# A four-layer gated cross-attention and FFN kernel on one core: packed rest matmuls, one-hot routing tile by tile, and two shared-expert tiles moved among the expert blocks

## The chip, the cores and the metric

The kernel runs on one core of a Trainium2 chip, in one launch. The metric is device time in microseconds (us). Beside unprofiled runs there is one profiled execution with a trace of every engine: PE (TensorE matmuls), PEld (TensorE weight loads, which overlap PE), DVE (VectorE), ACT (ScalarE), POOL (GpSimd) and SP, which only issues DMAs.

## The reference, cut to what matters

The stream x is 1024 tokens of 256 floats, eight tiles of 128 tokens. Four layers each add a gated attention and a gated FFN to it. All arithmetic is fp32 unless said otherwise. What the change touches is the attention of layer 0 and the expert FFNs of layers 0 and 3:

```
# layer 0 attention: 16 heads, rotary queries of 192, latent keys of 64
q_big  = rope((x @ Wq.T) per head @ w_kc_q)       # 192 a head
q_r    = q_big @ W_qr[h];  k_r = kv_r @ W_kr[h]   # 64 a head
x     += tanh(g) * (softmax(q_r @ k_r.T) @ kv_r @ w_kc_kv.T @ Wo.T)

# layer 0 FFN: 16 experts, 6 a token, and a shared expert
probs  = softmax(x @ gate_w.T);  idx = top_k(probs + gate_b, 6)
y      = sum over the chosen e of probs[e] * (silu(x@W1e.T+b1e) * (x@W3e.T+b3e)) @ W2e.T + ...
z      = silu(x @ ws1.T + bs1) * (x @ ws3.T + bs3) @ ws2.T + bs2
x     += tanh(g) * (y + z)

# layer 3 FFN: 8 experts, 2 a token, and a shared expert, without biases
```

## The kernel before, in words

**Queues.** Every engine executes its instructions in the order in which the built program holds them. That order comes from a scheduler: it follows the program text roughly, and it moves an operation ahead where it expects its inputs early. PSUM has two pools, `mm` (four banks) and `wide` (two pairs of banks).

**Layer 0's projections** (`attention0`, L647). `fold_scores0` (L468) multiplies W_qr and W_kr of each head into a matrix from the 192 rotary columns to the 64 latent ones, and splits it: `wide` holds the first 64 columns of each rotary half, `rest` the last 32, with zeros beside them, so that two heads share 128 output columns. The loop at L711 goes over four head groups f and two token groups g (eight units of three steps). `rotated(n)` multiplies xT by folded query weights (L407, four matmuls of 128x128 by 512), DVE multiplies by the rotary tables (L668), POOL adds (L676, L677). `to_latent(u)` (L680) applies `wide` in eight 64x64 matmuls. `rest_to_latent(u)` (L697) applies `rest` in four matmuls of 64 rows by 128 columns, and ACT copies the sums to SBUF.

**Layer 0's FFN** (`ffn0`, L1263). After two layernorms the normalised rows go to DRAM (`xd0`). `routing` (L1271) is a generator whose steps are taken between pieces of the shared expert: gate softmax and top six (`chosen`, L934), then `placed` (L985), which gives every (token, expert) pair a slot in blocks of 128 slots for one expert each. Its last part turns slots into token numbers with one-hot matrices: for each of the six picks DVE makes a hit matrix for all eight tiles at once (L1055, L1062, L1068, L1071), and PE adds them up in eight fp16 matmuls of 126 columns (L1073). From the sum DVE makes the gather and scatter indices (L1085 to L1089).

The shared expert runs over the eight tiles in three stages, `up` (L1283), `turn` (L1302), `down` (L1309), as `in_three` (L1256) staggers them; each tile ends in `gated_add` to x. Then `keep_rows` writes x to a sum in DRAM, `sums0[0]`.

**The blocks** (`Experts`, L1119; 55 in layer 0, 20 in layer 3). In iteration i, POOL gathers the rows of block i + 4 (`fetch`, L1137), PE transposes block i (`turn`, L1149), transposes the hidden of block i - 2 (L1204), does `up` of i - 1 (L1174, L1178, in layer 3 L1189) and `down` of i - 2 (L1213), and POOL scatters the result of i - 2 into one of two sums by turns, with addition in the DMA (L1225). Then `between(i)` puts other work in: every third block from i = 2 a step of `fold1` (L742, the folding of layer 1's attention weights: two steps at L753, one at L771, four at L784, four at L564, and a last one that only frees buffers), and after that steps of `ternary1` (L1439, DVE work for layer 1's FFN weights).

**Weights** pass through three buffers `C`; `used(name)` (L245) frees one and SP issues the load of the next.

**After the blocks** x is read back from `sums0[0]` in eight DMAs of 128 KB on SP, the other sum in four of 256 KB on ACT's queue, and DVE adds them (L1361) before layer 1's layernorm. At the end of the kernel the last sum is copied to the output in four DMAs (L1609).

## Time and profile before

| | |
|---|---|
| three runs | 974.55, 975.81, 976.93 us; median 975.81 |
| profiled execution | 984.07 us, of which the trace spans 982.3 |
| busy: PE, PEld, DVE, ACT, POOL | 860.7, 557.0, 527.7, 274.0, 343.7 us |
| mean granted PE clock | 0.931 of full speed |
| DMA | 75.12 MB in 40426 packets, mean 76 GB/s |

The stages that the change touches, in us from the span's start, read from the timeline:

| stage | from | to |
|---|---|---|
| layer 0's projections (`attention0`, the loop at L711) | 17 | 153 |
| shared expert and routing (`ffn0`) | 221 | 277 |
| layer 0's blocks, first gather to last scatter issued | 270.12 | 465.09 |
| reload of x, to layer 1's first transpose | 469.14 | 482.22 |
| layer 3's FFN, shared expert and blocks | 796 | 973 |
| copy to the output | 975.70 | 982.3 |

How to read it: a time is the busy time of one engine, and an idle engine costs nothing unless the others wait for it. A timeline row has start, duration, engine, source line, operation, output and inputs with their shapes, count, and in brackets the idle time before it and what ended that. A matmul of fp32 operands appears as two records; the end of a matmul is modelled, so the distance from one group's start to the next group's start is more reliable than a duration.

### The profile page before, as it was taken

How to read it: one execution, taken by the hardware profiler on the slowest of the kernel's cores; microseconds unless marked ns; L12 is line 12 of the kernel's file. 1: busy time of each engine (PE TensorE's matmuls, PEld its weight loads, DVE VectorE, ACT ScalarE, POOL GpSimd, SP SyncE). 2: the span in 40 equal slices, each digit the busy share in tenths (PEclk: the TensorE clock that was granted, in tenths of full speed). 3: DMA queues.
4: the chain of work that ended last, by engine and by line, in shares of the span. 5: the costliest groups of instructions: out<-in, count | busy, mean ns of one | idle time of the engine just before them, and what ended most of it. 6: DMA issues, size and time to landing. Idle time of an engine off the chain costs nothing.

```text
span 982.3 us, 12516 instructions
## 1 busy us (share of the span) xinstructions
PE 860.7 (88%) x4389; PEld 557.0 (57%) x4389; DVE 527.7 (54%) x1261; ACT 274.0 (28%) x531; POOL 343.7 (35%) x260
## 2 busy tenths in 40 slices
PE   5999998999999998985399988988637889999994
PEld 3544335876767876763247863745424656566662
DVE  3656455756934445461427748958786846222220
ACT  2211013334222232221113437024303532122221
POOL 0445451310067786786003127104101302144421
PEclk9999999999989999998599999979858979999998
DMA  9200217301166667555720000440000011122222
GB/s 354 81 15 11 88 34 232 89 22 30 54 156 163 126 151 168 80 84 64 245 99 1 1 1 27 162 144 1 22 0 1 2 43 51 44 44 44 39 27 60
DMA packets 40426, 75.12 MB, mean 76 GB/s; under 512 B 6369, under 2 KB 28883, under 8 KB 38987
## 3 DMA queue, kind: packets, MB, share of 16 engines
q1 hardware_dynamic: 24426, 51.99, 15.7%
q0 software_dynamic: 14496, 20.47, 12.8%
q10 hardware_dynamic: 1440, 1.84, 0.5%
q8 instruction: 39, 0.64, 0.3%
q14 instruction: 25, 0.20, 0.1%
HBM read 58.70 MB, written 16.61 MB: 77 GB/s over the span
## 4 chain that ended last, share of the span: by engine, by line
PE 34%; DVE 11%; ACT 3%; POOL 1%; issue 1%; DMA 1%; POOLq 0%; ACTq 0%; DVEq 0%
PE wide L1189 7%; PE mm L407 5%; PE mm L1213 3%; PE wide L1389 3%; PE mm L642 2%; PE mm L1520 2%; PE mm L437 2%; PE mm L915 1%; PE mm L1410 1%; PE mm L392 1%; DVE mx L884 1%; DVE big L1436 1%; PE wide L873 1%; DVE attn L886 1%; DVE sm L421 1%; DVE big L1437 1%
## 5 line engine op out<-in xcount | busy, mean ns | idle before, releaser
L423 POOL TENSOR_TENSOR attn<-attn,sm 128x1024 f32<-128x1024 f32 x32 | 60.8, 1901 | 245.8 <-DVE sm L422 227.2
L1198 DVE SCALAR_TENSOR_TENSOR blk<-wide,weight,blk 128x176 f32<-128x176 f32 (+1 forms) x75 | 37.0, 493 | 133.6 <-ACT blk L1197 130.7
L1225 POOL DMA_INDIRECT sums<-ring,big x55 | 87.8, 1596 | 32.1 <-issue 15.7
L668 DVE TENSOR_TENSOR rope<-wide,big 128x512 f32<-128x512 f32 x96 | 59.6, 684 | 57.1 <-PE wide L407 55.6
L407 PE MATMUL wide<-xT,big 128*128 128x512 f32 x192 | 88.6, 609 | 0.3 <-ACT big L542 0.3
L1178 PE MATMUL wide<-big,blk 128*128 x220 | 76.5, 469 | 0.0
L1137 POOL DMA_INDIRECT xs<-xd,big x55 | 54.8, 997 | 55.4 <-PE mm L1318 35.8
L1189 PE MATMUL wide<-big,blk 128*128 x160 | 72.2, 593 | 0.5 <-DVE blk L1150 0.5
L392 PE MATMUL mm<-ident,xn 128*128 128x128 f32 x112 | 24.7, 376 | 53.4 <-DVE xn L380 41.1
L1197 ACT ACTIVATE blk<-wide 128x176 f32<-128x176 f32 (+1 forms) x75 | 29.4, 392 | 121.8 <-PE wide L1189 60.2
L407 PEld LDWEIGHTS wide<-xT,big 128*128 128x128 f32 x192 | 35.6, 193 | 48.5 <-issue 38.7
L642 PE MATMUL mm<-vo,attnT 128*128 128x256 f32 x256 | 60.5, 390 | 0.9 <-ACT attnT L438 0.9
L1213 PE MATMUL mm<-big,blk 88*128 x220 | 57.7, 385 | 0.8 <-ACT blk L1206 0.5
L642 PEld LDWEIGHTS mm<-vo,attnT 128*128 128x128 f32 x256 | 48.5, 195 | 9.5 <-ACT attnT L438 3.3
L392 PEld LDWEIGHTS mm<-ident,xn 128*128 128x128 f32 x112 | 18.2, 189 | 62.3 <-ACT rstd L375 31.7
L438 ACT COPY attnT<-mm 128x512 f32<-128x512 f32 x64 | 35.0, 588 | 66.2 <-PE mm L437 66.2
L1213 PEld LDWEIGHTS mm<-big,blk 88*128 88x128 f32 x220 | 41.9, 192 | 16.7 <-ACT blk L1206 1.5
L1178 PEld LDWEIGHTS wide<-big,blk 128*128 128x128 f32 x220 | 40.3, 194 | 12.9 <-issue 0.8
L437 PE MATMUL mm<-ident,attn 128*128 128x128 f32 x256 | 36.9, 292 | 11.5 <-POOL attn L423 11.5
L442 DVE SCALAR_TENSOR_TENSOR x<-mm,tg,x 128x256 f32<-128x256 f32 x48 | 22.9, 477 | 44.7 <-PE mm L642 19.8
L421 DVE TENSOR_REDUCE sm<-attn 128x16 f32<-128x1024 f32 x32 | 38.9, 1215 | 14.7 <-ACT attn L415 12.6
L1137 POOL DMA_INDIRECT xs<-xd,scratch x20 | 19.4, 972 | 76.9 <-PE mm L1149 51.9
(330 smaller groups left out, 1690.4 us busy)
## 6 DMA issues: line engine op xcount, KB each, us to landing
big<-in_L_w_gate_up SPq DMA_DIRECT2D x8, 1024.0 KB
big<-in_L_w SPq DMA_DIRECT2D x4, 1408.0 KB
big<-in_L_w_down SPq DMA_DIRECT2D x8, 512.0 KB
w_L_qk<-in_L_qk SPq DMA_DIRECT2D x4, 896.0 KB
big<-in_L_w SPq DMA_DIRECT2D x4, 704.0 KB
big<-in_L_wo SPq DMA_DIRECT2D x1, 2048.0 KB
xd<-xn SPq DMA_DIRECT2D x16, 128.0 KB
sums<-x SPq DMA_DIRECT2D x16, 128.0 KB
```

The costliest lines, as they stand in the source:

```text
L392: nc.tensor.transpose(ps[:, i * P : (i + 1) * P], n[:, c * P : (c + 1) * P], ident)
L407: nc.tensor.matmul(ps, w(c), xT[:, c, :], start=(c == 0), stop=(c == 1))
L421: nc.vector.tensor_reduce(sm, e, AX.X, ALU.add)
L423: nc.gpsimd.tensor_tensor(e, e, sm.unsqueeze(2).to_broadcast([P, groups, n]), ALU.mult)
L437: nc.tensor.transpose(ps[:, i * P : (i + 1) * P], ev[:, pr * P : (pr + 1) * P], ident)
L642: nc.tensor.matmul(ps[:, :D], aT[:, s, :], vo[:, s, :], start=(s == 0), stop=(s == NP - 1))
L668: nc.vector.tensor_tensor(m[:, s, :].rearrange("q (b t) -> q b t", t=S), ps[:, s, :].rearrange("q (b t) -> q b t", t=S), table, ALU.mult,)
L1137: nc.gpsimd.indirect_dma_start(out=xs, out_offset=None, in_=self.xd, in_offset=bass.IndirectOffsetOnAxis(ap=self.gather[:, b : b + 1].bitc ...
L1178: nc.tensor.matmul(ps[:, 0, : 2 * n], st[:, c * P : (c + 1) * P], self.w[:, bass.ds(r + c * 2 * n, 2 * n)], start=False, stop=(c == 1),)
L1189: nc.tensor.matmul(ps[:, k, :n], st[:, c * P : (c + 1) * P], self.w[:, bass.ds(r + (2 * c + k) * n, n)], start=(c == 0), stop=(c == 1),)
L1213: nc.tensor.matmul(ps[:, :D], hT[:, j * P : (j + 1) * P], self.w[: self.chunk, bass.ds(r + j * D, D)], start=(j == 0), stop=(j == self.n - 1),
L1225: nc.gpsimd.indirect_dma_start(out=self.sums[b % len(self.sums)], out_offset=bass.IndirectOffsetOnAxis(ap=self.scatter[:, b : b + 1].bitca ...
```

## The change

It has five parts.

1. `rest` loses its zero half. Both token groups of one f now run together: `rest_to_latent(f)` issues 16 matmuls of 32 rows by 64 columns, at eight places of the array, into four PSUM banks. For token group 1 the two heads of a pair change places in the 128 latent rows (`half = i ^ g`), and the values of the second half of the tokens are stored swapped to match. The six steps of one f are taken in the order `turns`.
2. The hit matrices are made tile by tile: one TENSOR_SCALAR for the slot's row, one that compares the block and multiplies by the token number (up to 1024, in fp16). The one-hot matmuls have 63 columns.
3. The last two of the eight shared tiles are issued among blocks 1 to 6, one piece (`up`, `turn` or `down`) a block; their results are kept in SBUF (`later`) and added after the blocks. The folding's steps start at block 10 instead of 2, the ternary steps after block 45, two a block. L0_s13 and L0_s2 are freed after the last shared piece.
4. x is one tile of SBUF. In layer 0 the rows in DRAM are ordered with the eight tokens of one partition side by side, so that x and the second sum come back in two DMAs each with 4 KB pieces, and DVE adds 512 columns at once.
5. The output copy's access pattern has rows of 4 KB.

```diff
-        for n in range(3 * len(units) + 2):
+        turns = [(0, 0), (1, 0), (2, 0), (2, 1), (0, 1), (1, 1)]
...
+        for n in range(6 * NQ + 2):
+            f, m = divmod(n, 6)
...
+            if m == 3 and f < NQ:
+                to_latent(f, 0)
+            if m == 5:
+                rest_to_latent(f)
+            if m == 1 and f >= 1:
+                to_latent(f - 1, 1)
...
-        def rest_to_latent(u):
-            f, g = units[u]
-            pss, qr = sums.pop(u), made.pop(3 * u + 2)
+        def rest_to_latent(f):
+            sums[f, 1] = [ps_mm() for _ in range(2)]
+            qrs = [made.pop(6 * f + 2 + g) for g in range(NG)]
             for s in range(2):
-                for up in range(2):
-                    rows = slice(up * 64, (up + 1) * 64)
-                    nc.tensor.matmul(pss[up], rest[rows, f, s, :], qr[rows, s, :], start=False, stop=(s == 1))
+                for g in range(NG):
+                    for i in range(2):
+                        for up in range(2):
+                            lo, half = up * 64 + i * 32, i ^ g
+                            nc.tensor.matmul(
+                                sums[f, g][up][half * DC : (half + 1) * DC, :],
+                                rest[lo : lo + 32, f, s, :],
+                                qrs[g][lo : lo + 32, s, :],
+                                start=(s == 0 and g == 1),
+                                stop=(s == 1 and g == 0),
+                                tile_position=(lo, half * DC),
+                            )
...
-            nc.vector.tensor_tensor(
-                h,
-                place.unsqueeze(1).to_broadcast([P, NT, P]),
-                off[:, ts].unsqueeze(2).to_broadcast([P, NT, P]),
-                ALU.is_equal,
-            )
...
+            for t in range(NT):
+                m = k * NT + t
+                nc.vector.tensor_scalar(h[:, t, :], place, off[:, m : m + 1], None, ALU.is_equal)
+                nc.vector.tensor_scalar(
+                    v[:, t, :], block16[:, :nb], blk[:, m : m + 1], number[:, t : t + 1], ALU.is_equal, ALU.mult
+                )
...
+            if t < LATER:
+                gated_add(t, ps[:, :D], gate)
+            else:
+                nc.vector.tensor_scalar(later[:, t - LATER, :], ps[:, :D], gate, None, ALU.mult)
...
-        in_three(NT, up, turn, down)
+        in_three(LATER, up, turn, down)
...
         def between(i):
-            if i % 3 == 2 and not ended:
+            if shared:
+                if i:
+                    f, t = shared.pop(0)
+                    f(t)
+                if not shared:
+                    used("L0_s13")
+                    used("L0_s2")
+            elif i > 9 and i % 3 == 1 and not ended:
...
-            if i > 32 and ended:
+            for _ in range(2 if ended and i > 45 else 0):
                 next(ternary, None)
...
         for t in range(NT):
-            nc.sync.dma_start(out=x[t], in_=sums0[0][t * P : (t + 1) * P, :])
+            if t % TPG == 0:
+                tiles = slice(t, t + TPG)
+                nc.sync.dma_start(out=stream[:, tiles, :], in_=tiled(sums0[0], 0)[:, tiles, :])
+                more = t4([P, TPG, D], "more")
+                nc.scalar.dma_start(out=more, in_=tiled(sums0[1], 0)[:, tiles, :])
             if t % 2 == 0:
...
+                done = nc.vector.tensor_tensor(stream[:, two, :], stream[:, two, :], more[:, its, :], ALU.add)
+                if t >= LATER:
+                    mine = slice(t - LATER, t - LATER + 2)
+                    done = nc.vector.tensor_tensor(stream[:, two, :], stream[:, two, :], later[:, mine, :], ALU.add)
```

More of the change, by code (lines that the diff above doesn't have):

```diff
@@ L59 @@
 K3 = 2
+LATER = 6
 def _blocks(experts, keep):
@@ L76 @@
 C_SLOTS = 3
-FIXED = 2 * DC + 8 + 2 * E0 + E0 + 8 + 2 * E3 + 4 + 1 + NB0 + 8 + 1 + L + 2 + 1
-FIXED16 = P + NT + P + E0 * E0
+FIXED = 2 * DC + 8 + 2 * E0 + E0 + 8 + 2 * E3 + 4 + NB0 + 8 + 2 * NT + 1 + L + 2 + 1
+FIXED16 = P + NB0 + P + E0 * E0
 @with_exitstack
@@ L134, in evacuate @@
             nc.vector.tensor_copy(dst, src)
-    x = [const.tile([P, D], F32, tag=f"x{t}", name=f"x{t}") for t in range(NT)]
+    stream = const.tile([P, NT, D], F32, tag="x", name="x")
+    x = [stream[:, t, :] for t in range(NT)]
     big = const.tile([P, BIG], F32, tag="big", name="big")
@@ L174, in tile_flamingo @@
     which = take(4)
-    row1 = take(1)
     block = take(NB0)
     full = take(8)
+    number0, number3 = take(NT), take(NT)
     expert_of = take(1)[:96]
@@ L183, in tile_flamingo @@
     place = take(P, left16)
-    tile_of = take(NT, left16)
+    block16 = take(NB0, left16)
     before = take(P, left16)
@@ L359, in zeroed, with tiled, keep_rows @@
         nc.sync.dma_start(out=rows.rearrange("(p r) d -> p (r d)", p=P), in_=zeros[:, : rows.shape[0] * D // P])
-    def keep_rows(sums):
+    def tiled(rows, layer):
+        order = "(p t) d -> p t d" if layer == 0 else "(t p) d -> p t d"
+        return rows[:T].rearrange(order, t=NT)
+    def keep_rows(sums, layer):
         for t in range(NT):
-            nc.sync.dma_start(out=sums[t * P : (t + 1) * P, :], in_=x[t])
+            nc.sync.dma_start(out=tiled(sums, layer)[:, t, :], in_=x[t])
     def layernorm(g):
@@ L473, in fold_scores0 @@
         wide = wqk[:, :1024].rearrange("p (f i s d) -> p f i s d", f=NQ, i=2, s=2)
-        rest = wqk[:, 1024:].rearrange("p (f s i d) -> p f s i d", f=NQ, s=2, i=2)
-        nc.gpsimd.memset(rest, 0.0)
+        rest = wqk[:, 1024:1536].rearrange("p (f s d) -> p f s d", f=NQ, s=2)
         rT = w_rk0[:, : NP * CQ].rearrange("r (h q) -> r h q", h=NP)
@@ L516, in fold_scores0 @@
                     evacuate(
-                        rest[rows, fs, :, i, :],
+                        rest[rows, fs],
                         rests[up][rows, :256].rearrange("p (f s d) -> p f s d", f=2, s=2),
                     )
-        return wide, rest.rearrange("p f s i d -> p f s (i d)")
+        return wide, rest
     def fold_queries0(f):
@@ L594, in latents, with latent_attend @@
         return [t[:, g] for g in range(NG)]
-    def latent_attend(qcT, wvo, gate):
+    def latent_attend(qcT, wvo, gate, swapped=False):
         vos: dict = {}
@@ L616, in values @@
                 for j, ps in enumerate(pss):
-                    evacuate(v[:, 2 * r : 2 * r + 2, j, :], ps.rearrange("p (q o) -> p q o", q=2))
+                    evacuate(v[:, 2 * r : 2 * r + 2, (1 - j) if swapped and b >= B // 2 else j, :], ps.rearrange("p (q o) -> p q o", q=2))
             vos[b] = v.rearrange("p q j o -> p (q j) o")
@@ L652, in attention0 @@
         ring = region("weff", 2048, "rotated").rearrange("p (i s t) -> p i s t", i=2, s=2)
-        units = [(f, g) for f in range(NQ) for g in range(NG)]
+        turns = [(0, 0), (1, 0), (2, 0), (2, 1), (0, 1), (1, 1)]
         made: dict = {}
@@ L657, in rotated @@
         def rotated(n):
-            u, k = divmod(n, 3)
-            f, g = units[u]
+            f, m = divmod(n, 6)
+            k, g = turns[m]
             ps = ps_wide()
@@ L678, in rotated, with to_latent @@
             made[n] = qr
-        def to_latent(u):
-            f, _ = units[u]
-            pss = sums[u] = [ps_mm() for _ in range(2)]
-            qrs = [made.pop(3 * u + i) for i in range(2)]
+        def to_latent(f, g):
+            if not g:
+                sums[f, g] = [ps_mm() for _ in range(2)]
+            pss = sums[f, g]
+            qrs = [made.pop(6 * f + 4 * g + i) for i in range(2)]
             for s in range(2):
                 for i in range(2):
+                    half = i ^ g
                     for up in range(2):
@@ L689, in to_latent, with finished @@
                         nc.tensor.matmul(
-                            pss[up][i * DC : (i + 1) * DC, :],
+                            pss[up][half * DC : (half + 1) * DC, :],
                             wide[rows, f, i, s, :],
                             qrs[i][rows, s, :],
-                            start=(s == 0),
-                            stop=False,
-                        )
-        def rest_to_latent(u):
-            f, g = units[u]
-            pss, qr = sums.pop(u), made.pop(3 * u + 2)
-            for s in range(2):
-                for up in range(2):
-                    rows = slice(up * 64, (up + 1) * 64)
-                    nc.tensor.matmul(pss[up], rest[rows, f, s, :], qr[rows, s, :], start=False, stop=(s == 1))
-            for up in range(2):
-                last.append(nc.scalar.copy(qcT[g][:, 2 * f + up, :], pss[up]))
+                            start=(s == 0 and g == 0),
+                            stop=(s == 1 and g == 1),
+                        )
+            if g:
+                finished(f, g)
+        def rest_to_latent(f):
+            sums[f, 1] = [ps_mm() for _ in range(2)]
+            qrs = [made.pop(6 * f + 2 + g) for g in range(NG)]
+            for s in range(2):
+                for g in range(NG):
[10 more added lines that the diff above has]
+                            )
+            finished(f, 0)
+        def finished(f, g):
+            for up, ps in enumerate(sums.pop((f, g))):
+                last.append(nc.scalar.copy(qcT[g][:, 2 * f + up, :], ps))
         wide = None
@@ L710, in attention0 @@
         output = fold_output(w_kv0, [lambda: (w_o0, NH, lambda: None)])
-        for n in range(3 * len(units) + 2):
-            u, k = divmod(n, 3)
-            if n == 1:
+        for n in range(6 * NQ + 2):
+            f, m = divmod(n, 6)
+            if n == 2:
                 xT.append(transposed(layernorm(1)))
-            if u < len(units):
+            if f < NQ:
                 rotated(n)
-                if k == 1 and u % 2 == 0 and u // 2 + 1 < NQ:
-                    fold_queries0(u // 2 + 1)
-                if k == 1 and u >= len(units) - 4:
+                if m == 1 and f + 1 < NQ:
+                    fold_queries0(f + 1)
+                if m % 3 == 1 and f >= NQ - 2:
                     next(output)
@@ L722, in attention0 @@
                 wide, rest = fold_scores0()
-            if k == 0 and u >= 1:
-                to_latent(u - 1)
-            if k == 1 and u >= 1:
-                rest_to_latent(u - 1)
+            if m == 3 and f < NQ:
[4 more added lines that the diff above has]
+                to_latent(f - 1, 1)
             if n >= 6:
@@ L738, in attention0 @@
             load_experts0(e, e + 4)
-        latent_attend(qcT, wvo, gate)
+        latent_attend(qcT, wvo, gate, swapped=True)
         load_experts0(12, 16)
@@ L983, in chosen, with placed @@
         return cw, gated, mask
-    def placed(mask, n, keep, nb, stride, cut, keeping):
+    def placed(mask, n, keep, nb, stride, number, cut, keeping):
         order = [cut([P, NT, 8 + n]) for _ in range(2)]
@@ L1048, in placed @@
         hit = [cut([P, NT, P], F16) for _ in range(2)]
-        val = [cut([P, NT, 2, nb], F16) for _ in range(2)]
+        val = [cut([P, NT, nb], F16) for _ in range(2)]
         ps = ps_mm()
-        src = ps[:, : 2 * nb]
+        src = ps[:, :nb]
         for k in range(keep):
             h, v = hit[k % 2], val[k % 2]
-            ts = slice(k * NT, (k + 1) * NT)
-            nc.vector.tensor_tensor(
-                h,
-                place.unsqueeze(1).to_broadcast([P, NT, P]),
-                off[:, ts].unsqueeze(2).to_broadcast([P, NT, P]),
-                ALU.is_equal,
-            )
-            is_in = v[:, :, 0, :]
-            nc.vector.tensor_tensor(
-                is_in,
-                block[:, :nb].unsqueeze(1).to_broadcast([P, NT, nb]),
-                blk[:, ts].unsqueeze(2).to_broadcast([P, NT, nb]),
-                ALU.is_equal,
-            )
-            nc.vector.tensor_tensor(
-                v[:, :, 1, :], is_in, tile_of.unsqueeze(2).to_broadcast([P, NT, nb]), ALU.mult
-            )
-            nc.vector.tensor_scalar(is_in, is_in, row1, None, ALU.mult)
+            for t in range(NT):
[4 more added lines that the diff above has]
+                )
             for t in range(NT):
@@ L1075, in placed @@
                     h[:, t, :],
-                    v[:, t].rearrange("p a b -> p (a b)"),
+                    v[:, t],
                     start=(k == 0 and t == 0),
@@ L1080, in placed @@
             yield
-        row = cut([P, nb])
         none = cut([P, nb])
@@ L1084, in placed @@
         gather = keeping([P, nb], I32)
-        nc.vector.tensor_copy(row, src[:, :nb])
-        nc.vector.scalar_tensor_tensor(row, src[:, nb:], float(P), row, ALU.mult, ALU.add)
-        nc.vector.tensor_scalar(none, row, 0.0, spare, ALU.is_equal, ALU.mult)
-        nc.vector.scalar_tensor_tensor(scatter, row, -1.0, none, ALU.add, ALU.add)
+        nc.vector.tensor_scalar(none, src, 0.0, spare, ALU.is_equal, ALU.mult)
+        nc.vector.scalar_tensor_tensor(scatter, src, -1.0, none, ALU.add, ALU.add)
         nc.vector.tensor_scalar(gather, scatter, T - 1, None, ALU.bitwise_and)
@@ L1105, in placed, with stored @@
         return gather, scatter, expert, offset, used_blocks
-    def stored(normal, name, n):
-        xd = dram.tile([T, D + n], F32, tag=name, name=name)
+    def stored(normal, layer, n):
+        xd = dram.tile([T, D + n], F32, tag=f"xd{layer}", name=f"xd{layer}")
         for g, xn in enumerate(normal):
@@ L1112, in stored, with with_weights @@
                 t = g * TPG + i
-                nc.sync.dma_start(out=xd[t * P : (t + 1) * P, :D], in_=n)
+                nc.sync.dma_start(out=tiled(xd, layer)[:, t, :D], in_=n)
         return xd
-    def with_weights(xd, gated):
-        nc.sync.dma_start(out=xd[:, D:].rearrange("(t p) e -> p t e", p=P), in_=gated)
+    def with_weights(xd, layer, gated):
+        nc.sync.dma_start(out=tiled(xd, layer)[:, :, D:], in_=gated)
     class Experts:
@@ L1265, in ffn0 @@
         xT = [xt for xt, _ in normal]
-        xd = stored([xn for _, xn in normal], "xd0", E0)
+        xd = stored([xn for _, xn in normal], 0, E0)
         work, places = big[:, X0W : BIG - 400], Carver(big[:, BIG - 400 :])
@@ L1273, in routing @@
             route.append(cw)
-            with_weights(xd, gated)
-            route.append((yield from placed(mask, E0, K0, NB0, W0, cut, places)))
+            with_weights(xd, 0, gated)
+            route.append((yield from placed(mask, E0, K0, NB0, W0, number0, cut, places)))
         steps = routing()
@@ L1321, in down @@
             nc.tensor.matmul(ps[:, :D], cwT, b2_0, start=False, stop=True)
-            gated_add(t, ps[:, :D], gate)
-        in_three(NT, up, turn, down)
+            if t < LATER:
[3 more added lines that the diff above has]
+        in_three(LATER, up, turn, down)
         for _ in steps:
             pass
-        used("L0_s13")
-        used("L0_s2")
-        keep_rows(sums0[0])
+        keep_rows(sums0[0], 0)
         placing = route[1]
@@ L1336, in hTs @@
             return st[:FC0, 432:688]
+        later = work[:, : (NT - LATER) * D].rearrange("p (t d) -> p t d", d=D)
         fold = fold1()
@@ L1340, in ffn0 @@
         ternary = ternary1()
+        shared = [(f, t) for t in range(LATER, NT) for f in (up, turn, down)]
         def between(i):
-            if i % 3 == 2 and not ended:
+            if shared:
[6 more added lines that the diff above has]
+            elif i > 9 and i % 3 == 1 and not ended:
                 try:
@@ L1354, in ffn0 @@
         for t in range(NT):
-            nc.sync.dma_start(out=x[t], in_=sums0[0][t * P : (t + 1) * P, :])
-            if t % 2 == 0:
-                more = t4([P, 2, D], "more")
-                nc.scalar.dma_start(
-                    out=more, in_=sums0[1][t * P : (t + 2) * P, :].rearrange("(t p) d -> p t d", t=2)
-                )
-            done = nc.vector.tensor_tensor(x[t], x[t], more[:, t % 2, :], ALU.add)
+            if t % TPG == 0:
[3 more added lines that the diff above has]
+                nc.scalar.dma_start(out=more, in_=tiled(sums0[1], 0)[:, tiles, :])
+            if t % 2 == 0:
+                two, its = slice(t, t + 2), slice(t % TPG, t % TPG + 2)
+                done = nc.vector.tensor_tensor(stream[:, two, :], stream[:, two, :], more[:, its, :], ALU.add)
+                if t >= LATER:
+                    mine = slice(t - LATER, t - LATER + 2)
+                    done = nc.vector.tensor_tensor(stream[:, two, :], stream[:, two, :], later[:, mine, :], ALU.add)
         load_experts3(0, EARLY3, done)
@@ L1368, in ffn3 @@
         xT = [xt for xt, _ in normal]
-        xd = stored([xn for _, xn in normal], "xd3", E3)
+        xd = stored([xn for _, xn in normal], 3, E3)
         cut = Carver(*(region(tag, 2048, "scratch3") for tag in ("weff", "wqk")))
@@ L1374, in routing @@
             _, gated, mask = yield from chosen(xT, gate3, E3, K3, None, gate, 0, cut)
-            with_weights(xd, gated)
-            route.append((yield from placed(mask, E3, K3, NB3, W3, cut, cut)))
+            with_weights(xd, 3, gated)
+            route.append((yield from placed(mask, E3, K3, NB3, W3, number3, cut, cut)))
         steps = routing()
@@ L1417, in ffn3 @@
         used("L3_sd")
-        keep_rows(sums3[0])
+        keep_rows(sums3[0], 3)
         hidden = region("wvo", 2048, "hidden3")
@@ L1607, in tile_flamingo @@
         rows = slice(i * T // 4, (i + 1) * T // 4)
+        to, of = (v[rows].rearrange("(p r) d -> p (r d)", r=4) for v in (out, sums3[0]))
         engine = nc.scalar if i % 2 else nc.sync
-        engine.dma_start(out=out[rows], in_=sums3[0][rows])
+        engine.dma_start(out=to, in_=of)
 def _rope(length, dim):
@@ L1706, in _fixed @@
         row // 16 % 4 == np.arange(4),
-        row + 1,
         np.arange(NB0),
         P * np.arange(8),
+        NT * row + np.arange(NT) + 1,
+        row + P * np.arange(NT) + 1,
         row % 32,
@@ L1716, in _fixed @@
         np.arange(P),
-        np.arange(NT),
+        np.arange(NB0),
         row < np.arange(P),
```

## The prediction

> **What bounds the kernel now.** I read the page first, then busy time by stage, then the timeline of each stage that the diff touches. The chain of waits reaches back only to 481.57 us, where x is reloaded from DRAM; of the half of the span before it, where most of this change lies, it says nothing. There I go by stages.

> ```profile
> 17.00:151.00 134.00, 133.65 (x597) 60.02 (x600) 72.74 (x123) 20.95 (x56) 59.09 (x48) 0.99 0.22 76
> 277.00:283.00 6.00, 5.50 (x14) 2.96 (x14) 2.03 (x12) 0.32 (x1) 3.48 (x4) 0.50 0.85 235
> 388.00:442.00 54.00, 48.45 (x225) 35.31 (x224) 30.84 (x99) 14.99 (x43) 41.13 (x31) 0.97 0.56 102
> ```

> Columns: stretch, its length, then busy us of PE, PEld, DVE, ACT, POOL; granted clock, DMA share, GB/s. Layer 0's projections (17 to 151) are PE's alone: 133.65 of 134 us. The start of layer 0's blocks (277 to 283) ran at half clock. Late blocks (388 to 442) leave PE 5.5 us idle; there POOL is the bound, as its timeline shows:

> ```profile
> 270.12 1.14 POOL L1137 DMA_INDIRECT xs<-xd,big  x1 [35.81 <-PE mm L1318]
> ...
> 407.70 1.59 POOL L1225 DMA_INDIRECT sums<-ring,big  x1 [0.30 <-ACT blk L1206]
> 409.60 0.98 POOL L1137 DMA_INDIRECT xs<-xd,big  x1 [0.31 <-PE mm L1149]
> 410.89 1.60 POOL L1225 DMA_INDIRECT sums<-ring,big  x1 [0.30 <-issue]
> ...
> 463.54 1.55 POOL L1225 DMA_INDIRECT sums<-ring,big  x1 [0.63 <-issue]
> ```

> One gather and one scatter per block, with about 0.30 us between any two: 410.89 - 407.70 = 3.19 us a block, whatever PE does. PE's own need, read from consecutive Silus on ACT (L1197), is 2.65 us a block; a block with a full step of layer 1's folding takes 4.67, with one of the last four 3.8. Three blocks with a full step are 9.97 us of PE against 9.57 of POOL. So PE leads by a little until the folding's seventh step, POOL afterwards.

> **1. Projections: the rest rows, two groups in one.** PE's timeline of one unit:

> ```profile
> 43.15 3.70 PE L407 MATMUL wide<-xT,big 128*128 128x512 f32 x8
> 46.78 1.99 PE L703 MATMUL mm<-rotated,wqk 64*128 64x512 f32 x8
> 48.70 1.55 PE L407 MATMUL wide<-xT,big 128*128 128x512 f32 x3
> ```

> Each fp32 matmul is two records. L407's four full ones take 46.78 - 43.15 = 3.63 us, 0.91 each. L703's four use 64 rows, run two at a time, and take 48.70 - 46.78 = 1.92 us: two rounds. There are two such groups for each of four f, 3.84 us per f. The change makes one group of 16 matmuls of 32 rows by 64 columns per f. Eight such tiles fill the array; if all eight run at once it is again two rounds, 1.92 us, and 4 x 1.92 = **7.7 us** go. DVE (72.74 of 134) and POOL (59.09) do not take over; the number of PSUM copies stays.

> The trace has no 32-row tile. The nearest row is the folding of the scores, where 64-row tiles go from 64 to 32 columns:

> ```profile
> 22.59 1.15 PE L488 MATMUL mm<-big 64*64 64x64 f32 x32
> 23.67 0.67 PE L502 MATMUL mm<-big 64*32 64x64 f32 x32
> ```

> The same 16 matmuls take 0.67 instead of 1.15 us: eight tiles at once do run, 1.7 times as fast as four. [...] a bank gets tile rows 0 to 31 in one column half and rows 32 to 63 in the other. If such pairs take turns, it is four rounds, 3.84 us, and nothing is gained. Bounds: -8 to +42.9 (all 16 in turn: 4 x (16 x 0.91 - 3.84)). I take the row: within one column half, all four row tiles go to four different banks[...]. The step is **-7.7**. The dropped memset (POOL L475, 0.94 us at the start) hides behind the first loads.

> **2. Routing tile by tile.** Of each pick, four wide operations become sixteen small ones:

> ```profile
> L1055 DVE TENSOR_TENSOR big<-fixed,big 128x1024 f16<-128x1024 f16 x6 | 7.3, 1213 | 0.0
> L1062 DVE TENSOR_TENSOR big<-fixed,big 128x504 f16<-128x504 f32 x6 | 4.1, 676 | 0.0
> L1068 DVE TENSOR_TENSOR big<-big,fixed 128x504 f16<-128x504 f16 x6 | 4.0, 668 | 0.0
> L1071 DVE TENSOR_SCALAR big<-big,fixed 128x504 f16<-128x504 f16 x6 | 2.1, 348 | 0.0
> ```

> Now: 1.213 + 0.676 + 0.668 + 0.348 = 2.91 us a pick, less 0.09 of overlap at each of four starts, 2.55; six picks 15.3 us. After: 96 TENSOR_SCALARs of 128 or 63 elements. Near rows: 0.18 (L1043, 48 wide; L1103, 63 wide) to 0.25 us (L1087), less 0.09 of overlap: 0.09 to 0.16 each, 8.6 to 15.4 us in all. I take 0.13, 12.5 us: 2.8 us gained. PE's 48 one-hot matmuls halve in width, under 1 us together. Layer 3 does two picks under a PE that is busy all through (25.00 of 25 us from 800 to 850): nothing.

> **3. Two shared tiles and the folding moved into the blocks.** A shared tile costs PE 2.67 us up (246.02 to 248.69 in its timeline), 0.6 for transposes, about 2.9 down (270.36 to 273.49 to 276.18): 6.2; two are 12.4. PE ends the shared part at 277.0, so then at 264.6. Routing's last operation L1089 ended at 269.23. In the built program's DVE order the hit loop begins behind the same six shared products as before, at 248.1; plus 12.5, three gated adds (0.39 each), half a microsecond for the last matmul and 1.6 for the index arithmetic: 263.9. The first gather then starts at 264.8 instead of 270.12. A gather takes 2.9 us to land (issued 442.35, used 445.26): block 0 has its rows at 267.7. Tile 6's up, 2.67 us, which the built order puts just ahead, fills PE until then. With 2.7 us for transpose, copy and up, block 0's Silu comes at 270.4, against 282.42.

> Then it is paid back. Blocks 0 to 9 are PE's: 9 x 2.65 + (12.4 - 2.7) = 33.6 us, so block 9's Silu is at 304.0 against 312.15: 8.1 earlier. After block 9 seven full folding steps follow instead of four: 3 x (9.97 - 9.57) is 1.2 us more. The ternary work on DVE now lies in blocks 50 to 54 instead of 43 to 48; where it slowed PE before (block 44 took 4.85 us), POOL lagged enough to hide it. Near the end it hides less: about 1 us. Net -5.9.

> The clock can spoil this. [...] But in the row of 277 to 283 the clock was 0.50 although PE lacked only 0.4 us in 274 to 277; a half-rate window of that length, about 6.8 us, costs 3.4: -2.5. I take **-4.5** for steps 2 and 3 together, range -9 to +3.

> What the moved steps issue: SP frees L0_s13 and L0_s2 only after tile 7, near 299 us, so L1_qk0 (768 KB) lands near 305, and folding step 1 at block 10 wants it near 307. Cover is 2 us; if it is late, PE waits in order and every block behind it with it. The loads of L1_w1 and L1_w2 move along with the folding; DVE's reduction already waits for them (1.3 and 2.4 us), and the built order puts the reductions two blocks behind them again: same.

> **4. 4 KB pieces.** The reload of x and the second sum:

> ```profile
> 477.89 0.42 DVE L1361 TENSOR_TENSOR x<-x,more 128x256 f32<-128x256 f32 x1 [0.43 <-DMA x<-sums]
> ...
> 481.66 1.38 DVE L380 TENSOR_SCALAR xn<-x,mv,rstd 128x256 f32<-128x256 f32 x4
> ```

> From 471 to 477 the DMA engines were 87 to 99% busy at 302 to 314 GB/s with 1 KB pieces; the start of the kernel (8 to 20 us) shows 396 to 439 GB/s with larger ones, so the last data may come up to 1 us earlier. But they come in two lumps, and behind the second DVE has three 512-wide adds (0.61 each, doubling L1361) where it had two or three of 0.34: 1.1 us more. Net **+0.8**, -0.5 to +1.5. The row order within xd and the sums changes no piece size of gather or scatter. The last copy (975.70 to 982.3) moves 0.52 MB in 64 packets per queue, 8 KB each already: 0.

> **Sum.** -7.7 - 4.5 + 0.8 = -11.4 us. The profiled execution took 984.07 us (span 982.3): 972.7, a ratio of 0.9884. On the median of the runs, 975.81, that is **964.5 us**; its own range is 957 to 970.

> **Rivals.** (a) Banks shared by row tiles take turns: step 1 is worth 0, -3.7 in all, **972**. [...] against it L502. (b) The blocks' ramp gains nothing: 0.2 us per small DVE operation makes the loop 19 us, PE waits 6 us for routing at half clock, and the 9.7 us of moved work come on top: +2, in all -4.9, **971**. For it the half clock at 277; against it the small rows of DVE. (c) The slower end: the 16 tiles of the rest group run mostly one after another, since each loads its own weights. Place: four times in 17 to 151, where PE has no slack. Break-even is 3.84 + 3.7/4 = 4.77 us a group, over five rounds; eight rounds (7.3) give 972.1 + 13.8 = **986**, sixteen 1015. For it: no 32-row tile in the trace. Against it: L502. (d) a and b together, +2.8: 979.

> **Chances.** Forecast 0.45, a 0.20, b 0.12, c 0.16, d 0.07. A measurement of this kernel can tell 0.2%, 2 us, from no change. Faster: the forecast and nearly all of a and b, 0.72; slower: c and most of d, 0.22; same 0.06. The range 955 to 980 leaves out c's upper part and a little below.

> **What would show it.** Step 1: the rest group (L718) in about 1.9 us; 3.8 is rival a, over 4.8 rival c. Step 2: the small operations' start-to-start near 0.13. Step 3: first gather near 265 (on before's clock, less step 1), ten blocks in some 34 us, full clock at the ramp, L1_qk0 not waited for, last scatter's distance to the first gather near 194 us (193.4 now). Step 4: xn about 4.9 us behind the last data instead of 3.8. A folding step or tile 7 waiting on a load would make the forecast wrong, as would a group of 32-row tiles that is not eight wide.

## The result and the profile after

The changed kernel takes 988.5 us (median of 4 runs, 985.31 to 994.14), the kernel before 975.96; the ratio is 1.0136, 95% interval 1.0087 to 1.0185. It is slower by about 13 us, where 11 us of gain had been forecast. All ratios leave out single executions that took over 1.5% longer than the fastest of the same kernel. The profiled execution took 987.41 us, span 985.5, mean granted clock 0.918.

The profile after, first the rest group of the projections in PE's timeline:

```profile
50.46 0.66 PE L718 MATMUL mm<-rotated,wqk 32*64 32x512 f32 x4
...
52.36 7.13 PE L415 MATMUL wide<-xT,big 128*128 128x512 f32 x16
```

The group of 32-row tiles runs from 50.46 to 52.36: 1.90 us, eight tiles at once. PE reaches layer 0's latent values 8.9 us earlier than before. That gain is there, and it is gone by the first gather of the blocks. The page's rows of the granted clock, before and after, each digit a fortieth of the span:

```profile
PEclk9999999999989999998599999979858979999998
```

```profile
PEclk8999999998589999999599999979858979999998
```

The new thing is `858` at the tenth to twelfth place, some 222 to 296 us: the end of layer 0's shared expert and the start of its blocks. A table by stretches of the changed kernel (columns as in the prediction: busy us of PE, PEld, DVE, ACT, POOL, then clock, DMA share, GB/s):

```profile
226.00:236.80 10.80, 9.80 (x48) 6.12 (x46) 10.26 (x49) 1.93 (x5) 0.00 (x0) 1.00 0.10 21
236.80:239.40 2.60, 0.06 (x1) 0.00 (x0) 2.60 (x9) 0.47 (x1) 0.00 (x0) 1.00 0.00 0
240.00:280.00 40.00, 37.56 (x127) 23.41 (x126) 20.88 (x106) 3.61 (x9) 4.24 (x5) 0.50 0.09 27
281.00:321.00 40.00, 37.75 (x202) 27.68 (x201) 13.58 (x53) 10.69 (x31) 25.14 (x21) 1.00 0.53 112
```

PE idles from 236.8 to 239.4. Then its clock is at half for 41 us, from 239.8 to 280.8, and nearly all of that time it is busy (37.56 of the 40 us in the table). PE's timeline shows what it waited for:

```profile
234.33 2.53 PE L1304 MATMUL wide<-w_L_s,xT 128*128 128x352 f32 x8
239.41 0.20 PE L1088 MATMUL mm<-big 128*128 128x63 f16 x1 [2.55 <-DVE big L1083]
239.45 0.54 PE L1317 MATMUL mm<-ident,shared 128*88 128x128 f32 x3
```

L1304 is the up stage of the last tile of six. Behind it stands the first one-hot matmul (L1088), which waits 2.55 us for DVE's first hit matrix. The transposes and down stages behind it (L1317, L1325) had their inputs, the last of them from DVE at 235.90, and started only behind it, at 239.45: PE ran them in order. Before, two more up stages stood there, 5.3 us of PE, and the wait was 0.57; in the kernel before:

```profile
252.09 0.62 PE L1073 MATMUL mm<-big 128*128 128x126 f16 x8 [0.57 <-DVE big L1071]
```

While PE waits in the changed kernel, DVE is busy with routing steps that lie ahead of its loop (2.60 of 2.60 us in the table). The loop itself starts at 238.90:

```profile
238.90 0.30 DVE L1084 TENSOR_SCALAR big<-fixed,big,fixed 128x63 f16<-128x63 f16 x1
...
239.64 0.25 DVE L1083 TENSOR_SCALAR big<-fixed,big 128x128 f16<-128x128 f16 x1
239.80 0.29 DVE L1084 TENSOR_SCALAR big<-fixed,big,fixed 128x63 f16<-128x63 f16 x1
240.01 0.25 DVE L1083 TENSOR_SCALAR big<-fixed,big 128x128 f16<-128x128 f16 x1
```

From start to start a pair takes 240.01 - 239.64 = 0.37 us (0.163 + 0.205); 48 pairs are 17.6 us, where the four wide operations come to 15.3 by the prediction's sum. From 255 on DVE even waits for the slow PE (0.60 us at 256.76). The first gather in POOL's timeline:

```profile
274.55 1.15 POOL L1149 DMA_INDIRECT xs<-xd,big  x1 [49.55 <-PE mm L1333]
```

Set beside the kernel before (us; minus is earlier):

| mark | before | after | difference |
|---|---|---|---|
| PE reaches layer 0's latent values | 155.1 | 146.2 | -8.9 |
| first operation of the one-hot loop | 248.2 | 238.9 | -9.3 |
| first gather | 270.12 | 274.55 | +4.4 |
| Silu of block 0 | 282.42 | 282.54 | +0.1 |
| Silu of block 9 | 312.15 | 317.20 | +5.1 |
| last scatter | 463.54 | 468.99 | +5.5 |
| layer 1's xn | 481.66 | 488.01 | +6.4 |

Between the loop's start and the first gather 13.8 us are lost.

### The profile page after: what moved, and what is told of

The parts are those of the page before. It is cut to its first block, busy times and chain, and to the rows that moved or that the text cites. A ratio compares the mean times of both kernels' runs of the same rounds, so it can differ in the third digit from the quotient of the medians.

```text
span 985.5 us, 12697 instructions
## 1 busy us (share of the span) xinstructions
PE 864.5 (88%) x4451; PEld 560.7 (57%) x4453; DVE 533.6 (54%) x1350; ACT 274.6 (28%) x531; POOL 342.9 (35%) x259
## 5 line engine op out<-in xcount | busy, mean ns | idle before, releaser
L1149 POOL DMA_INDIRECT xs<-xd,big x55 | 54.6, 992 | 66.3 <-PE mm L1333 49.5
L1225 PE MATMUL mm<-big,blk 88*128 x220 | 57.8, 385 | 2.0 <-ACT blk L1218 2.0
L1225 PEld LDWEIGHTS mm<-big,blk 88*128 88x128 f32 x220 | 41.9, 192 | 18.1 <-ACT blk L1218 3.8
L1190 PEld LDWEIGHTS wide<-big,blk 128*128 128x128 f32 x220 | 39.6, 190 | 13.2 <-issue 1.1
L1149 POOL DMA_INDIRECT xs<-xd,scratch x20 | 19.5, 975 | 77.5 <-PE mm L1161 53.9
L1201 PEld LDWEIGHTS wide<-big,blk 128*128 128x128 f32 x160 | 28.8, 190 | 28.9 <-issue 28.2
```

The source lines that it names most:

```text
L1149: nc.gpsimd.indirect_dma_start(out=xs, out_offset=None, in_=self.xd, in_offset=bass.IndirectOffsetOnAxis(ap=self.gather[:, b : b + 1].bitc ...
L1190: nc.tensor.matmul(ps[:, 0, : 2 * n], st[:, c * P : (c + 1) * P], self.w[:, bass.ds(r + c * 2 * n, 2 * n)], start=False, stop=(c == 1),)
L1201: nc.tensor.matmul(ps[:, k, :n], st[:, c * P : (c + 1) * P], self.w[:, bass.ds(r + (2 * c + k) * n, n)], start=(c == 0), stop=(c == 1),)
L1225: nc.tensor.matmul(ps[:, :D], hT[:, j * P : (j + 1) * P], self.w[: self.chunk, bass.ds(r + j * D, D)], start=(j == 0), stop=(j == self.n - 1),
```

## The experiments

**Theory.** The two tiles that moved away took with them the work that covered DVE's first pick. PE idles, the clock halves, and then what is left of the shared expert runs at half rate. **Rivals:** it is DVE's loop alone; it is the many short waits among the interleaved one-hot matmuls; the packing loses its gain by itself further on. Ratios are to the kernel before, with their 95% intervals.

| kernel | ratio | interval | mean clock of the same runs |
|---|---|---|---|
| e1_pack_alone | 0.9918 | 0.9892-0.9945 | 0.934 |
| e3_eight_shared | 0.9980 | 0.9960-1.0001 | 0.932 |
| e2_wide_onehot | 1.0007 | 0.9970-1.0043 | 0.926 |
| e4_grouped | 1.0060 | 1.0034-1.0085 | 0.924 |
| e9_dense | 1.0024 | 1.0005-1.0044 | 0.931 |
| e8_cover | 0.9943 | 0.9917-0.9968 | 0.935 |
| e7_cover_small | 1.0045 | 1.0028-1.0062 | 0.925 |
| e5_eight_wide | 0.9923 | 0.9897-0.9949 | 0.937 |
| e6_eight_wide_rows | 0.9899 | 0.9866-0.9933 | 0.936 |
| the change | 1.0136 | 1.0087-1.0185 | 0.919 |

**1. The packing alone** (`fold_scores0`, `attention0`, the swapped values; nothing else).

> The kernel before with step 1 alone (rest rows of two token groups in one packed matmul group). Theory (packing is worth what the trace of the changed kernel shows, four groups of 1.90 us fewer, and everything behind moves up by it): 975.8 - 7.7 = 968 us, ratio 0.992, first gather near 262.3 on POOL. Rival (the gain is lost further on by itself, in a load or a clock window): over 972 us.

Measured: 0.9918, 8.0 us faster; first gather at 261.49. Step 1 is worth what was forecast, and nothing takes it back.

**2. Eight shared tiles ahead of the blocks again**, and the folding from block 2 on (step 3 undone). The rest of the change stays.

```diff
-LATER = 6
+LATER = 8
...
-            elif i > 9 and i % 3 == 1 and not ended:
+            if i % 3 == 2 and not ended:
...
-            for _ in range(2 if ended and i > 45 else 0):
+            if i > 32 and ended:
                 next(ternary, None)
```

> The changed kernel with all eight tiles of the shared expert ahead of the blocks again and the folding from block 2 on (step 3 undone), one-hot matrices still tile by tile. Theory (the two moved tiles took away the two up stages, 5.3 us of PE, that covered DVE's first pick): PE waits under 1 us at the first one-hot matmul, the granted clock stays at 1.00 through the loop, first gather near 264, time 968 to 973. Rival (interleaving 48 one-hot matmuls that each wait for DVE is enough to halve the clock, whatever lies ahead): clock 0.50 in the loop, 980 to 990.

Measured: 0.998. The table by stretches:

```profile
238.00:256.00 18.00, 18.00 (x114) 12.44 (x112) 18.00 (x95) 3.81 (x9) 0.00 (x0) 1.00 0.05 15
```

PE is busy 18.00 of 18 us at full clock, with most of the 48 one-hot matmuls strewn among the shared ones as in the change; its longest wait for a hit matrix is 0.18 us. So interleaving by itself doesn't halve the clock, and that rival falls. The first gather comes at 260.71, 13.8 us earlier than in the change. The median, 975.1 us, lies above the 968 to 973 that were expected; experiment 6 says what the small operations have to do with it.

**3. Wide one-hot operations, and small ones with the matmuls in groups.** In the first, three wide operations a pick replace the sixteen; in the second the first one-hot matmul of a pick also waits for the pick's last small operation.

```diff
-            for t in range(NT):
-                m = k * NT + t
...
+            nc.vector.tensor_tensor(
+                h,
+                place.unsqueeze(1).to_broadcast([P, NT, P]),
+                off[:, ts].unsqueeze(2).to_broadcast([P, NT, P]),
+                ALU.is_equal,
+            )
...
+            nc.vector.tensor_tensor(v, v, number.unsqueeze(2).to_broadcast([P, NT, nb]), ALU.mult)
```

> The changed kernel with the one-hot matrices of a pick made by three wide operations on DVE (as before, without the two value planes) instead of sixteen small ones. The order on PE then has a pick's eight one-hot matmuls together. Theory (the loss is PE's clock: PE runs out of shared work ahead of the first one-hot matmul and the many short waits between one-hot matmuls keep it at half rate for 41 us): PE still idles, some 4 us, ahead of the first pick, the clock halves, but comes back after two or three windows (7 to 10 us) since PE now runs 2 to 3 us without a wait; first gather 262 to 267, time 973 to 979. Rival (it is only DVE's loop, 17.6 us of small operations against 13.7 of wide ones): 4 us better than the changed kernel, 984. Second rival (the first idle alone decides, and the clock stays down as long as PE waits for DVE at all): 985 to 990.

> The changed kernel with its small DVE operations, but the first one-hot matmul of each pick also waits for the pick's last small operation, so that PE gets the eight together and not one by one among the shared matmuls. Theory (short waits keep the clock down): PE idles 5 us at the first pick and the clock halves there, then PE has 2 to 3 us of unbroken work between picks and the clock returns within 10 to 15 us; first gather 265 to 270, 976 to 983. Rival (DVE's 2.9 us a pick leave PE waiting each time and that keeps the clock down as well): 985 to 990, first gather 272 or later.

Measured: 1.0007 and 1.0060. Both let PE idle longer at the first pick (4.51 and 5.13 us), as expected. The first meets its numbers (median 976.9 us, first gather at 265.53), the second misses them (983.4, 272.69). In the traces of both the clock does not come back within the expected 7 to 10 and 10 to 15 us. With wide operations, the wait, then the table by stretches:

```profile
240.56 0.61 PE L1096 MATMUL mm<-big 128*128 128x63 f16 x8 [4.51 <-DVE big L1094]
...
240.60:270.60 30.00, 30.00 (x117) 20.68 (x117) 14.61 (x25) 3.34 (x8) 4.03 (x4) 0.50 0.10 30
276.60:296.00 19.40, 19.14 (x89) 13.65 (x88) 7.30 (x27) 5.39 (x15) 9.70 (x8) 1.00 0.36 66
```

PE is busy 30.00 of 30 us, with no wait at all, and stays at half rate. Short waits are therefore not needed to hold the clock down, and that part of my theory fell. In this profile it returned at about 276, some 2 us into the next up stage (tile 6, from 273.9). The profiled executions of both kernels (983.68 and 988.35 us) are slower than their medians, and those with wide operations differ much among themselves: the fastest took 971.4 us at a mean clock of 0.938, the slowest in the ratio 985.3 at 0.919, and time and clock correlate at -0.93. In the faster ones the clock must have been down for less time, but no trace shows where. Expressed as time at half rate, 2 x (1 - clock) x span (in the traces of before and after the clock is at 1.00 or at 0.50, never between), one microsecond of it goes with 0.36 us of time; in the other kernels with 14 executions or more it goes with 0.20 to 0.40.

**4. A dense burst.** What brings the clock back? The wide version again, with eight up matmuls of 128x128 by 352 added (`dense`), behind a pick, whose result nobody reads:

```diff
         def turn(t):
+            if t == 3:
+                dense()
```

> The wide one-hot run again (two tiles moved, PE idle ahead of the first pick, clock at half for 36 us), with two more up stages put in behind the third pick: eight fp32 matmuls of 128x128 by 352 whose result nobody reads, on top of the work the kernel needs. Theory (at half rate only dense matmuls over all 128 rows bring the clock back; the shared expert's 88-row and 18-row ones do not): the clock is back at 1.00 within 7 us of the burst's start, and the gain (half of what is left of the loop, some 8 us) about pays for the burst: first gather 263 to 268. Rival (the clock comes back on its own time, or when DVE's loop is over): it stays at 0.50 until 276 or later, and the burst adds 5 to 9 us: first gather 271 to 275, ratio 1.006 to 1.010.

Measured: 1.0024. PE's timeline shows the burst and the first down stage behind it; beside it the same down stage in the version without a burst:

```profile
248.47 7.27 PE L1330 MATMUL wide<-w_L_s,xT 128*128 128x352 f32 x16
...
255.95 1.97 PE L1354 MATMUL mm<-w_L_s,shared 88*128 88x256 f32 x8
```

```profile
248.61 3.62 PE L1333 MATMUL mm<-w_L_s,shared 88*128 88x256 f32 x8
```

The clock is back at 253.1, 4.7 us into the burst, and stays at 1.00 to about 273: the down stage takes 1.97 instead of 3.62 us. The first gather comes at 264.21 in spite of the burst. The rival (the clock returns on its own time) does not fit this trace; it is one trace against one, since the executions without a burst differ as well. The burst also displaced an up stage, so PE idled 6.98 us at the first pick, and in time it gained nothing: 1.0024 against 1.0007, with overlapping intervals.

**5. Cover for the first pick.** Two tiles moved as in the change, but a pick's one-hot matmuls are emitted and pinned behind a down stage, so that a turn and a down stage stand ahead of the first; once with wide operations, once with the change's small ones. In the diff `mm` is the last matmul of a down stage, and `picks` holds the one-hot matmuls of finished picks.

```diff
+            behind.append(mm)
+            while picks:
+                picks.pop(0)()
```

> The changed kernel with two tiles moved, three wide one-hot operations a pick, and the one-hot matmuls of a pick emitted behind a down stage of the shared expert and pinned there, so that one turn and one down stage (3.5 us of PE) stand ahead of the first one-hot matmul. Theory (the first idle of PE is what halves the clock, and the shared turn and down stages never bring it back): PE idles about 1 us at the first pick, the clock stays at 1.00 through the loop, first gather 256 to 260, time 962 to 968, ratio 0.986 to 0.991. Rival (PE's turn and down stages are too light to hold the clock once the up stages are through): clock 0.50 from about 245, ratio 1.000.

> The changed kernel with all its parts and its small DVE operations; only the one-hot matmuls of a pick are emitted behind a down stage of the shared expert and pinned there, so that one turn and one down stage stand ahead of the first one-hot matmul on PE, as in the run with cover and wide one-hot operations (ratio 0.9943). Theory (the first idle of PE is what cost the changed kernel its clock, and the small operations cost what DVE's loop is longer by, 17.6 against 13.7 us, no more): PE idles 1 to 2 us at the first pick, at most two half-rate windows in the loop, first gather 260 to 264, ratio 0.997 to 1.002. Rival (with small operations PE waits so often for DVE between one-hot matmuls that the clock stays at half rate in spite of the cover): clock 0.50 through the loop, first gather 270 or later, ratio 1.008 to 1.014.

Measured: 0.9943 and 1.0045. With wide operations:

```profile
240.43 0.41 PE L1084 MATMUL mm<-big 128*128 128x63 f16 x8 [2.14 <-DVE big L1114]
...
242.50:245.90 3.40, 3.40 (x18) 2.66 (x17) 2.52 (x5) 0.00 (x0) 0.00 (x0) 0.51 0.11 39
246.00:259.40 13.40, 11.32 (x79) 7.92 (x78) 10.54 (x21) 2.13 (x6) 1.14 (x1) 1.00 0.11 38
```

PE still idles 2.14 us, where 1 had been expected. The clock is at half for one spell of 3.4 us in the loop (242.5 to 245.9) and again at 259.5 to 263, and the first gather comes at 258.24; the ratio is 0.6% above the middle of what was expected. With small operations the wait at the first pick is only 0.20 us and the clock holds. Then it falls in a second place, as the table by stretches shows:

```profile
240.00:250.00 10.00, 8.40 (x55) 5.71 (x55) 10.00 (x55) 2.39 (x6) 0.00 (x0) 1.00 0.04 13
250.40:253.00 2.60, 1.25 (x12) 0.65 (x11) 2.60 (x13) 0.00 (x0) 0.00 (x0) 0.92 0.00 0
253.40:273.00 19.60, 18.02 (x56) 11.20 (x55) 8.57 (x45) 1.09 (x3) 4.93 (x5) 0.50 0.18 55
```

From 250.4 to 253.0 the built order has ten one-hot matmuls in a row on PE; six are ready, and the last four come at DVE's pace of one every 0.37 us. Half rate then lasts 20 us instead of 41, and the ratio lies between that of full cover and that of the change. Neither number of the expectation was met. The cause shows twice: cover alone takes 0.9% off the change, and where PE is left at DVE's pace later on, for 2.6 us, it pays with 20 us of half rate.

**6. Eight tiles and wide operations** (the edits of experiments 2 and 3 together), **with and without step 4.**

```diff
-        order = "(p t) d -> p t d" if layer == 0 else "(t p) d -> p t d"
+        order = "(t p) d -> p t d"
```

(this and the reload in pieces of 1 KB in the second one only)

> The changed kernel with steps 2 and 3 undone at once: eight shared tiles ahead of the blocks, three wide one-hot operations a pick. What stays is the packing and step 4 (row order of layer 0's token buffers in DRAM, 4 KB pieces). Pack alone was 0.9918, eight shared tiles with small one-hot operations 0.998. Theory (the small operations are what costs the rest of that 0.6%): ratio 0.990 to 0.993. Rival (step 4 costs it: the new row order slows the scatters into the sums or their reload): 0.996 to 0.999.

> The kernel of the run with eight tiles and wide one-hot operations, with step 4 undone too (tokens in DRAM in their own order, x reloaded in eight and four DMAs of 1 KB pieces): packing, and three wide one-hot operations in place of four. Theory (step 4 is worth nothing or up to 1 us of loss): ratio 0.989 to 0.992, within 0.2% of the run that keeps step 4. Rival (step 4 costs 4 to 6 us): 0.5% below the run that keeps step 4.

Measured: 0.9923 and 0.9899. Against experiment 2 the first has only the one-hot operations changed, and is 0.57% faster, 5.6 us, with intervals that do not overlap; its first gather is 3.35 us earlier (257.36). That is the price of the small operations against three wide ones. Step 4 is 0.24% between the two, with overlapping intervals: not resolved. The second has the lowest ratio here, 9.9 us below the kernel before; it is not told apart from the packing alone.

## Why the prediction was wrong, by its steps

**Step 1, the packing: right.** -7.7 forecast; 1.90 us a group instead of 1.92, and -8.0 us alone (-5.4 to -10.5). Rival (a) is refuted: if row tiles that share a bank took turns, the group would have taken 3.84 us. In the new group rows 0 to 31 in one column half and 32 to 63 in the other write to the same bank, and all eight tiles still run at once: in PE's timeline eight records start within 0.03 us (four at 50.46, four at 50.49), and the next eight 0.48 us later. Rival (c), over 4.77 us, is refuted with it.

**Step 2, routing tile by tile: the size was off.** I took 0.13 us for a small operation, from rows of 48 and 63 columns with overlap taken off; the bounds were 0.09 to 0.16. Measured are 0.163 and 0.205 from start to start, the second one with two operands per partition: a loop of 17.6 instead of 12.5 us, by these sums 2.3 more than before instead of 2.8 less. Rival (b)'s 0.2 was nearer. At the first gather the 2.3 us do not show: with the clock at 1.00, the loop's first operation and the first gather lie 21.7 us apart (238.98 to 260.71 in experiment 2), against 21.9 in the kernel before. So the gain is missing, and little is lost there against the four wide operations of before. Against three wide ones the small ones cost 5.6 us (experiment 6).

**Step 3, the moved work: wrong, and it decides.** Two terms failed. First, "Tile 6's up, 2.67 us, which the built order puts just ahead, fills PE until then" looked at the gap ahead of block 0 and not at the one ahead of the first one-hot matmul, where the two up stages that moved had stood as cover. Experiment 2 puts them back, and the wait is gone with clock 1.00. Second, a fall of the clock was priced at one spell of 6.8 us, 3.4 us of loss; the spell at the start of the blocks in the kernel before has that length (276.5 to 283.4). In the change it lasted 41 us.

The ratios take the change apart: step 1 alone is -8 us, steps 2, 4 and 5 on top of it are +6 (0.9980 against 0.9918), and step 3 on top of those is +15 (1.0136 against 0.9980; some 10 to 20, since the change has only four runs). Together that is +13. Of the 15 us, 13.8 stand at the first gather already (274.55 against 260.71). What the clock has of them is an estimate: the executions of the change have a mean clock of 0.919, 160 us at half rate, those of experiment 2 0.932 and 133. At 0.36 us each the 27 us make 10, with the slopes of the other kernels 5 to 11. Where the 6 us of steps 2, 4 and 5 arise is open: the packing alone and experiment 2 reach block 9's Silu at 304.16 and 303.44 us, but their last scatter at 453.44 and 456.60.

The -5.9 counted on a clock that stays up with tile 6 in the gap; that was my estimate, and no trace had shown it. In the traces the clock fell after idles of 2.55 us (the change, at 239.8) and 2.14 us (experiment 5 with wide operations, at 242.4), and with wide operations alone it did not return in 30.00 us without a wait.

Nor does the move pay with the clock mostly repaired. In experiment 5 with wide operations, block 0's Silu comes 5.7 us earlier than with eight tiles ahead (265.06 against 270.72), block 9's only 0.3 earlier (299.65 against 299.95), and the last block's 2.0 later; the ratios, 0.9943 against 0.9923, are not told apart. Of the forecast's 8.1 at block 9 about half comes with a faster loop and eight tiles as well (299.95, against 304.16 with the packing alone); the gather does not come earlier for the move (258.24 against 257.36), since the end of DVE's loop sets it (254.60 and 254.02) and not PE. The forecast's 33.6 us for blocks 0 to 9 held (34.7). L1_qk0 was in time: the first folding step (317.91) shows no wait.

**Step 4, the reload: right in the trace, too small for the times.** From the last scatter's issue to xn it takes 19.0 us instead of 18.1: +0.9, forecast +0.8.

**The range**, 955 to 980, left out a clock that stays down. Rival (b), a PE that waits for routing at half clock, came nearest. It put the wait down to a longer loop, where the wait lay ahead of the loop's first matrix, and it was priced at +2 us, where step 3 cost some 15.

## What to carry to other kernels

When a change moves work away, ask of each instruction left behind what it stood in front of: the moved up stages were cover for DVE's first pick, and PE took its matmuls in order. Price a fall of the TensorE clock by what runs next, not by the idle time: behind 2.55 us of idling came 41 us at half rate, and the first gather was 13.8 us later than with the cover in place, since in those 41 us the stages that followed did not lift the clock again. Small operations on DVE should be priced from start to start in the same form, operands per partition included (0.163 and 0.205 us here), before many replace a few.

## What the hardware showed that was not expected

At full clock the shared turn and down stages (matmuls over 88 and 18 of 128 rows, and transposes) with the one-hot matmuls among them left it at 1.00. In the kernel before it was 24 us:

```profile
252.00:276.00 24.00, 23.35 (x147) 17.62 (x146) 16.88 (x36) 5.49 (x14) 4.66 (x5) 1.00 0.27 84
```

In experiment 5 with wide operations it was 246 to 259.4, though PE was busy for only 11.32 of 13.40 us. At half rate the same stages ran for long without a return: 30.00 us busy with wide operations, about 33 us with groups, 34 us in the change. With eight dense matmuls over 128 rows it was back in 4.7 us. In experiment 5 with wide operations it was back after 3.4 us (242.5 to 245.9), mainly of 88-row matmuls. What in PE's work decides on the return, these runs do not show.
